# Attention: where the older unit's sums stand among the scores of a slot

## The chip, the core and the metric

One Trainium2 chip, one of its cores. The time is the device time in microseconds of one execution of the kernel; the median of three runs is compared.

## What is computed

Two macaron layers over a sequence of 2048 rows of 256 features, each a half-weighted feed-forward network, an attention with 16 heads of 16 features, and a second half-weighted feed-forward network. The change is in the attention, which both layers use. Cut to what matters (the first layer; the second has rotary positions and biases in place of the distance term):

```python
attn = jnp.einsum('bhqd,bhkd->bhqk', q, k) / math.sqrt(HEAD_DIM)
attn = attn + alibi_bias(seq_len, N_HEADS)[None] + causal_mask(seq_len)[None, None]
attn = jax.nn.softmax(attn, axis=-1)
y = jnp.einsum('bhqk,bhkd->bhqd', attn, v)
y = y.transpose(0, 2, 1, 3).reshape(bsz, seq_len, n_embd)
return jnp.einsum('bsd,de->bse', y, W_o)
```

## The kernel before

The sequence is cut into four chunks `c` of 512 queries, and the heads into four quartets `g`. A *group* `n = 4c + g` is one quartet's attention for one chunk of queries, so there are 16 groups in a layer. A *slot* is a group and a block `kb` of 128 keys. Group `n` has `4(c + 1)` slots, since later keys are masked: 4 slots for groups 0 to 3, 8 for 4 to 7, 12 for 8 to 11, 16 for 12 to 15, 160 in all. The last four slots of a group (`t` = 0 to 3) lie on the diagonal. There the first `128t` queries are left out and a mask is added by a further small matmul.

For a slot the kernel does this:

- `st_pair` (L725): scores with the keys on the partitions, two heads at a time, into a pair of PSUM banks (`pst`, L733). The matmuls are bf16 on the whole 128x128 array. There are two such pairs.
- `exp_pair` (L746): one exponential on ScalarE for two heads, into `pT` (L753). Five such tiles are held.
- `av_part` (L759): the sums. Each head's `pT` is multiplied with the values and a column of ones, in fp32, into a quarter of the partitions of one accumulator bank, `acc` (the tile `pav`, L768): a 128x32 piece of the array for each head. The 512 queries are cut at `mid` in two halves, `part` 0 and 1. A half is 8 instructions for the four heads. On the diagonal the halves are shorter, and for `t` = 2 and 3 all the queries are in `part` 0.
- After `part` 0 of a diagonal slot, `divide` (L779) transposes 128 finished columns of `acc` on VectorE (`yt`, L789), takes the reciprocals of the row sums (`rd`, L793) and multiplies on GpSimd (`zt`, L794).

The exponential needs the maximum of its row, which is worked out earlier, from scores with the queries on the partitions. That is done by `mx_unit` (L663): one matmul for each head (`pq`, L671, with a mask at L679 on the diagonal), into one of three PSUM buffers, and one VectorE reduction (`mx`, L682). A *maximum unit* is four heads of one block of 128 queries against 512 keys. The units belong to the next group, or to the one after it on the diagonal, and a hand-written plan (`put`, L837 to L859) spreads them over the slots. Nearly all slots have one, and some in the first chunk and at the start of a group have two; the last 19 slots of a layer have none. When a group's maxima are complete, `mx_end` (L684) and `mx_turn` (L699) bring them into rows of `q`, with three small DMAs.

The order on TensorE, ScalarE, VectorE and GpSimd is the order in which the program issues its instructions; each engine takes them one after the other and waits on semaphores. The loop at L939 writes this order. In a slot with a maximum unit it takes the head pairs in the order 1, 0 (`hp`). For each it issues two scores, two maximum scores with their reductions, the exponential, and then some sums:

```python
sums(i - 2 + (hp == 0), hp)
```

`sums(i, part)` (L929) issues every half that is waiting, up to this one. So behind heads 2,3 comes `part` 1 of the slot before the last, and behind heads 0,1 comes `part` 0 of the last slot. In a slot with no maximum unit both pairs' scores come first, then both exponentials, then `sums(i - 1, 1)`: both halves of the last slot. Further maximum units of the slot come after the sums (L966), then what is due (`run_due`: the turned maxima, the back-transpose `z`, the output matmuls `pwo`), and a step of the preparations (projections `pp`, `dn`, values `pv`) or of a layernorm of the neighbouring stage.

Of the kernel before, what the change touches and what calls it, by code (L numbers as in the profile page):

```python
# [46 lines left out]
def macaron_kernel(ctx: ExitStack, tc: tile.TileContext, a, out):  # L47
# [139 lines left out]
    def draw(work):  # L187
        while work and next(work[0], "end") == "end":
            work.popleft()

    def pull():

        for work in list(background)[:2]:
            if next(work, "end") == "end":
                background.remove(work)
# [294 lines left out]
    def attention(layer, following):  # L490
# [9 lines left out]
        with ExitStack() as st:  # L500
# [91 lines left out]
            def prep_v(c):  # L592
                ready(c)
                for t in range(0, T, 2):
                    pp = ps_one(f"pv{layer}_{c}_{t}").rearrange("p (t f) -> p t f", t=2)
                    for i in range(2):
                        for dc in range(DC):
                            nc.tensor.matmul(  # L598
                                pp[:, i, :],
                                lhsT=xns[c][:, dc, (t + i) * P : (t + i + 1) * P],  # L600
                                rhs=wqkv[:, dc, 2 * E : 3 * E],
                                start=dc == 0,
                                stop=dc == DC - 1,
                            )
                    for i in range(2):
                        vs = va[c][:, t + i, 0 : H * VW].rearrange("p (h d) -> p h d", d=VW)[:, :, 0:D]
                        pv = pp[:, i, :].rearrange("p (h d) -> p h d", d=D)
                        if layer == 0:
                            nc.scalar.copy(vs, pv)
                        else:  # L610
                            nc.vector.tensor_tensor(
                                vs, pv, b_v.rearrange("p (h d) -> p h d", d=D), ALU.add
                            )
                    if t + 2 == T:
                        done.add(("v", c))
                    yield
# [108 lines left out]
            def st_pair(n, kb, hp, apart=False):  # L725

                c, g = divmod(n, G)
                kc, t = divmod(kb, T)
                lo = t * P if kc == c else 0
                pair, ps = banks(f"pst{layer}_{n}_{kb}_{hp}", apart)  # L730
                for i in range(2):
                    hh = 2 * hp + i
                    nc.tensor.matmul(  # L733
                        ps[i][:, lo:CH],
                        lhsT=ks[n, kc][0:rows, hh, t * P : (t + 1) * P],
                        rhs=qs[n][0:rows, hh, lo:CH],
                        start=True,
                        stop=kc < c,
                    )
                    if kc == c:  # L740
                        nc.tensor.matmul(  # L741
                            ps[i][:, lo : lo + P], lhsT=ident_b, rhs=mask_kq, start=False, stop=True
                        )
                return pair, ps

            def exp_pair(n, kb, hp, scores):  # L746
                pair, ps = scores
                c, g = divmod(n, G)
                kc, t = divmod(kb, T)
                lo = t * P if kc == c else 0  # L750
                pT = ap.tile([P, 2, CH], F32, tag="pT", bufs=5, name=f"pT{layer}_{n}_{kb}_{hp}")
                if pair is not None:
                    nc.scalar.activation(pT[:, :, lo:CH], pair[:, :, lo:CH], AF.Exp, scale=0.25)  # L753
                else:
                    for i in range(2):
                        nc.scalar.activation(pT[:, i, lo:CH], ps[i][:, lo:CH], AF.Exp, scale=0.25)
                return pT

            def av_part(n, kb, pTs, part):  # L759
                c, g = divmod(n, G)  # L760
                kc, t = divmod(kb, T)
                lo = t * P if kc == c else 0
                mid = (lo + CH) // 2 if CH - lo > CH // 2 else CH
                a, b = ((lo, mid), (mid, CH))[part]
                if a < b:
                    for hh in range(4):
                        v0 = (4 * g + hh) * VW
                        nc.tensor.matmul(  # L768
                            acc[hh * SLOT : (hh + 1) * SLOT, a:b],
                            lhsT=va[kc][:, t, v0 : v0 + SLOT],  # L770
                            rhs=pTs[hh // 2][:, hh % 2, a:b],
                            start=kb == 0 and part == 0,
                            stop=kb == (c + 1) * T - 1,
                            skip_group_check=True,
                        )
                if part == 0 and kc == c:
                    divide(n, t)
# [89 lines left out]
            def run_due(all_of=False):  # L867
                while True:
                    due = [x for x in later if all_of or x[0] <= now[0]]
                    if not due:  # L870
                        return
                    later.remove(due[0])
                    due[0][1](*due[0][2])
# [3 lines left out]
            def step():  # L877
                draw(preps)

            def need(*what):  # L880
                while what not in done:
                    assert preps, what
                    step()
# [6 lines left out]
            def mx_next(unit, heads):  # L890
                n, t, kc = unit
                mx_unit(n, t, kc, heads)
                if 3 in heads:
                    left[n] -= 1
                    if not left[n]:
                        mx_end(n)
                        at(1, mx_turn, n)
# [8 lines left out]
            def load_to(slot):  # L906
                while uses and uses[0][1] <= slot:
                    load(*uses.popleft()[0])
# [12 lines left out]
            def turned(n):  # L921
                if n % 2 == 1:
                    c, q = divmod(n // 2, G // 2)
                    at(2, turn_back, c, q)
                    if q == G // 2 - 1:
                        for dc in range(DC):
                            at(3 + dc, output, c, dc)

            def sums(i, part):  # L929

                while unsummed and unsummed[0][::2] <= (i, part):
                    _, unit, p = unsummed.popleft()
                    n, kb, _ = unit
                    need("v", kb // T)
                    av_part(*unit, p)
                    if p == 1 and kb == (n // G + 1) * T - 1:
                        turned(n)

            for i, (n, kb) in enumerate(slots):  # L939
                c = n // G  # L940
                if kb == 0 and n % G == 0 and 0 < c < NCH - 1:

                    preps.extend((prep_qk(c + 1, "k"), prep_qk(c + 1, "q"), prep_v(c + 1)))
                if n not in turned_max:
                    run_due(all_of=True)
                load_to(i + 3)
                units = maxima.get(i, [])
                pTs = [None, None]
                if units:
                    for hp in (1, 0):  # L950
                        ps = st_pair(n, kb, hp)
                        mx_next(units[0], (2 - 2 * hp, 3 - 2 * hp))
                        pTs[hp] = exp_pair(n, kb, hp, ps)
                        sums(i - 2 + (hp == 0), hp)
                else:


                    both = []
                    for hp in (1, 0):
                        both.append(st_pair(n, kb, hp, pairs[0] % 3 == 2))  # L960
                        pairs[0] += 1
                    for hp, ps in zip((1, 0), both):
                        pTs[hp] = exp_pair(n, kb, hp, ps)
                    sums(i - 1, 1)
                unsummed.extend((i, (n, kb, pTs), part) for part in range(2))
                for unit in units[1:]:  # L966
                    mx_next(unit, (0, 1, 2, 3))
                run_due()
                if preps and (c <= 1 or i % 2):
                    step()  # L970
                    if c == 0 and i % 2:
                        draw(background)
                else:
                    pull()
                now[0] += 1
# [37 lines left out]
    def begin(layer, following):  # L1013
        att = attention(layer, following)
        begun[:] = att, next(att)
# [149 lines left out]
```

## Time and profile before

| what | value |
|---|---|
| three runs | 1952.93, 1954.04, 1957.03 us |
| their median | 1954.04 us |
| the profiled execution | 1957.69 us |
| its span, first to last instruction | 1955.7 us |
| granted TensorE clock, mean | 0.960 |
| attention of layer 0 and of layer 1, about | 266 to 789 us, 1203 to 1762 us |

The span is 2 us shorter than the execution's own time. PE is TensorE, DVE is VectorE, ACT is ScalarE, POOL is GpSimd. A row of the timeline has the start in us, the length in us, the engine, the line, the operation with output and inputs, how many instructions are merged in it, and in brackets the idle time before it with what ended it. Matmuls overlap, so that the distance from start to start counts for TensorE, and not the sum of lengths.

### The profile page before, as it was taken

Reading aid. Unit: us, or ns where it says so; the run is one execution under the profiler, and the core shown is the slowest. Engines: PE = TensorE matmul, PEld = TensorE weight load, DVE = VectorE, ACT = ScalarE, POOL = GpSimd, SP = SyncE. Lnnn points to the kernel's source line nnn. Section 1 sums busy time; section 2 is a strip of 40 time slices with the busy share of each in tenths; the row PEclk is TensorE's granted clock in tenths of the full one; section 3 lists DMA queues with packets and bytes.
Section 4 is the critical chain, followed back from the end, with each engine's and each line's share of the span. In section 5 each row is a group of like instructions: output and inputs, shape, how many; then the busy total and the mean of one; then the engine's idle time right before and its main releaser. Section 6 shows DMA issues by size and latency. Waiting matters only on the chain. (4 is left out here: it accounts for less than half of the span.)

```text
span 1955.7 us, 26994 instructions
## 1 busy us (share of the span) xinstructions
PE 1761.4 (90%) x10684; PEld 726.5 (37%) x10684; DVE 1361.6 (70%) x2384; ACT 894.2 (46%) x1112; POOL 458.4 (23%) x418
## 2 busy tenths in 40 slices
PE   5699789999999999789999876898999999998997
PEld 1233344433433333333444333433333333333443
DVE  7866377787788883666575655868877888825664
ACT  4343254555555668334422312445555656673220
POOL 3455321101000000455453432211111000003422
PEclk9799899999999999989999986999999999999999
DMA  4000252213211000200000115222122110000000
GB/s 129 1 1 33 82 148 83 73 54 102 62 45 46 28 28 2 73 1 0 1 11 0 54 61 158 82 73 92 52 69 86 43 43 26 18 1 0 11 11 22
DMA packets 50510, 93.10 MB, mean 48 GB/s; under 512 B 5424, under 2 KB 33072, under 8 KB 50128
## 3 DMA queue, kind: packets, MB, share of 16 engines
q1 hardware_dynamic: 49296, 89.28, 14.8%
q10 hardware_dynamic: 1088, 2.10, 0.3%
q8 instruction: 84, 1.38, 0.3%
q14 instruction: 42, 0.34, 0.1%
HBM read 59.51 MB, written 27.26 MB: 44 GB/s over the span
## 5 line engine op out<-in xcount | busy, mean ns | idle before, releaser
L682 DVE TENSOR_REDUCE mx<-pq 128x1 f32<-128x512 f32 (+3 forms) x1280 | 708.6, 603 | 158.5 <-PE pq L679 91.2
L753 ACT ACTIVATE pT<-pst 128x1024 f32<-128x1024 f32 (+3 forms) x614 | 542.6, 896 | 334.9 <-PE pst L733 196.8
L671 PE MATMUL pq<-k,q 105*128 105x512 bf16 (+7 forms) x1280 | 378.8, 353 | 74.7 <-DVE mx L682 52.3
L733 PE MATMUL pst<-q,k 99*128 99x512 bf16 (+7 forms) x1280 | 357.7, 354 | 5.1 <-ACT pT L753 4.2
L768 PE MATMUL pav<-pT,va 128*32 128x256 f32 (+1 forms) x4608 | 352.4, 382 | 5.2 <-DVE yt L789 5.0
L281 PE MATMUL pg_f<-xn,wgu 128*128 128x512 f32 x512 | 229.8, 602 | 11.5 <-DVE hr_f L318 11.5
L794 POOL TENSOR_TENSOR zt<-yt,rd 128x64 f32<-128x64 f32 x128 | 38.4, 300 | 795.2 <-DVE rd L793 795.1
L733 PEld LDWEIGHTS <-k 105*128 105x128 bf16 (+1 forms) x1280 | 101.5, 98 | 254.1 <-issue 218.4
L317 ACT ACTIVATE sl_f<-pg_f 128x512 f32<-128x512 f32 x128 | 76.0, 594 | 251.8 <-PE pg_f L281 175.0
L671 PEld LDWEIGHTS <-q 105*128 105x128 bf16 (+1 forms) x1280 | 124.5, 100 | 148.0 <-issue 44.3
L306 PE MATMUL pg_f<-xn,wgu 128*128 128x512 bf16 x512 | 156.2, 413 | 19.5 <-DVE wgu L170 6.8
L768 PEld LDWEIGHTS pav<-pT,va 128*32 128x32 f32 x4608 | 93.8, 108 | 208.7 <-issue 174.8
L281 PEld LDWEIGHTS pg_f<-xn,wgu 128*128 128x128 f32 x512 | 98.6, 193 | 136.9 <-issue 121.0
L306 PEld LDWEIGHTS <-wgu 128*128 128x128 bf16 x768 | 77.7, 101 | 166.9 <-issue 74.7
L292 PE MATMUL po_f<-h_f,wd 128*128 128x512 f32 x256 | 116.3, 608 | 17.3 <-DVE h_f L418 17.3
L340 POOL TENSOR_TENSOR ss_f<-ss_f,sq_f 128x512 f32<-128x512 f32 x56 | 91.1, 1628 | 111.5 <-ACT sq_f L339 111.3
L679 PE MATMUL pq<-mask_qk,ident_b 128*128 128x128 bf16 x512 | 107.3, 227 | 0.0
L741 PE MATMUL pst<-mask_kq,ident_b 128*128 128x128 bf16 x512 | 103.1, 222 | 0.0
L306 PE MATMUL pg_f<-xm_f,wgu 128*128 128x512 bf16 x256 | 85.3, 416 | 14.0 <-DVE xm_f L238 14.0
L318 DVE TENSOR_TENSOR h_f<-sl_f,pg_f 128x512 f32<-128x512 f32 x64 | 43.6, 682 | 76.4 <-ACT sl_f L317 76.3
L789 DVE STREAM_TRANSPOSE yt<-pav 128x128 f32<-128x128 f32 x128 | 39.8, 311 | 76.7 <-PE pav L768 76.7
L394 DVE TENSOR_TENSOR ge_f<-h_f 128x1536 bf16<-128x1536 f32 (+2 forms) x48 | 67.6, 1437 | 28.0 <-ACT h_f L387 28.0
(132 smaller groups left out, 1802.5 us busy)
## 6 DMA issues: line engine op xcount, KB each, us to landing
k<-dk SPq DMA_DIRECT2D x80, 384.0 KB
dk<-p_k SPq DMA_DIRECT2D x48, 256.0 KB
dq<-p_q SPq DMA_DIRECT2D x48, 256.0 KB
q<-dq SPq DMA_DIRECT2D x32, 384.0 KB
x<-in_xT ACTq DMA_DIRECT2D x4, 512.0 KB
raw<-in_w_gu SPq DMA_DIRECT2D x8, 256.0 KB
wgu<-in_w_gu SPq DMA_DIRECT2D x1, 2048.0 KB
cs_k<-in_cos_sin SPq DMA_DIRECT2D x4, 512.0 KB
```

The source lines that it names most:

```text
L281: nc.tensor.matmul(pg[:, half, :], lhsT=wgu[:, dc, half * F + f * P : half * F + (f + 1) * P], rhs=xn[:, dc, :], start=dc == 0, stop=dc == ...
L292: nc.tensor.matmul(po, lhsT=w[:, f, dc * P : (dc + 1) * P], rhs=h[:, f, :], start=f == 0, stop=f == FC - 1,)
L306: nc.tensor.matmul(pg[:, half, :], lhsT=wgu0[:, dc, half * F + f * P : half * F + (f + 1) * P], rhs=xp[part][:, dc, :], start=part == 0 an ...
L317: nc.scalar.activation(sl, pg[:, 0, :], AF.Silu)
L340: nc.gpsimd.tensor_tensor(ss, ss, sq, ALU.add)
L671: nc.tensor.matmul(pq, lhsT=qs[n][0:rows, hh, t * P : (t + 1) * P], rhs=ks[n, kc][0:rows, hh, 0:w], start=True, stop=kc < c,)
L679: nc.tensor.matmul(pq[:, w - P : w], lhsT=ident_b, rhs=mask_qk, start=False, stop=True)
L682: nc.vector.tensor_reduce(mxs[n][:, t, hh, kc : kc + 1], pq, AX.X, ALU.max)
L733: nc.tensor.matmul(ps[i][:, lo:CH], lhsT=ks[n, kc][0:rows, hh, t * P : (t + 1) * P], rhs=qs[n][0:rows, hh, lo:CH], start=True, stop=kc < c,)
L741: nc.tensor.matmul(ps[i][:, lo : lo + P], lhsT=ident_b, rhs=mask_kq, start=False, stop=True)
L753: nc.scalar.activation(pT[:, :, lo:CH], pair[:, :, lo:CH], AF.Exp, scale=0.25)
L768: nc.tensor.matmul(acc[hh * SLOT : (hh + 1) * SLOT, a:b], lhsT=va[kc][:, t, v0 : v0 + SLOT], rhs=pTs[hh // 2][:, hh % 2, a:b], start=kb == ...
```

## The change

In a slot with a maximum unit, no sums are issued between the two head pairs. After both pairs, their maxima and their exponentials, `sums(i - 1, 1)` issues both halves of the last slot's sums together, as in the slots with no maximum unit, which are left as they were. No instruction is added or taken away.

```diff
                         ps = st_pair(n, kb, hp)
                         mx_next(units[0], (2 - 2 * hp, 3 - 2 * hp))
                         pTs[hp] = exp_pair(n, kb, hp, ps)
-                        sums(i - 2 + (hp == 0), hp)
                 else:
-
 
                     both = []
                     for hp in (1, 0):
...
                     for hp, ps in zip((1, 0), both):
                         pTs[hp] = exp_pair(n, kb, hp, ps)
-                    sums(i - 1, 1)
+
+                sums(i - 1, 1)
                 unsummed.extend((i, (n, kb, pTs), part) for part in range(2))
```

## The prediction

> **What bounds the kernel now.** I read the page first, then the two attention stretches in the table by windows, then the timeline of single slots, and last the table of waits.
>
> ```profile
> PE 1761.4 (90%) x10684; PEld 726.5 (37%) x10684; DVE 1361.6 (70%) x2384; ACT 894.2 (46%) x1112; POOL 458.4 (23%) x418
> ```
>
> TensorE is busy for 90% of the span. In the windows of the two attention stretches (266 to 789 us, 1203 to 1762 us) it is fuller still; the last quarter of layer 0 reads:
>
> ```profile
> 611.00:789.00 178.00, 173.69 (x1520) 62.97 (x1516) 120.03 (x227) 119.85 (x144) 4.70 (x16) 1.00 0.08 23
> ```
>
> The columns after the length are PE, PEld, DVE, ACT and POOL busy, then the granted clock (1.00). PE has 173.7 of 178 us; VectorE 120. So what changes PE's own sequence changes the time. Here is one half of an undisturbed slot, on the timeline:
>
> ```profile
> 728.21 0.59 PE L671 MATMUL pq<-k,q 105*128 105x512 bf16 x2
> 728.41 1.02 ACT L753 ACTIVATE pT<-pst 128x1024 f32<-128x1024 f32 x1 [0.46 <-PE pst L733]
> 728.62 1.29 DVE L682 TENSOR_REDUCE mx<-pq 128x1 f32<-128x512 f32 x2 [0.25 <-PE pq L671]
> 728.73 0.64 PE L768 MATMUL pav<-pT,va 128*32 128x256 f32 x8
> 729.30 0.61 PE L733 MATMUL pst<-q,k 105*128 105x512 bf16 x2
> ```
>
> Two maximum scores (pq), eight pav instructions (one half of a unit's sums), two scores (pst). PE never waits: a half takes 1.54 us, a slot 3.08. VectorE has 0.25 us to spare in each half. From starts: pq to pav 0.52, pav to the next pst 0.57.
>
> **The change part by part.** No instruction is added or removed; no DMA, and no position in SP's queue, is touched. In a slot with a maximum unit, the half behind heads 2,3 goes, and behind heads 0,1 both halves of the unit one slot older stand together. Three things follow on PE and one on VectorE.
>
> *1. Fewer changes between score and sum matmuls: a gain.* The last group's slots (no maxima) already have both halves together:
>
> ```profile
> 759.31 1.07 PE L768 MATMUL pav<-pT,va 128*32 128x256 f32 x16
> ...
> 760.32 1.04 PE L733 MATMUL pst<-q,k 105*128 105x512 bf16 x4
> ```
>
> Sixteen pav instructions take 1.01 us to the next pst, two times eight take 2 x 0.57 = 1.14: 0.13 saved. The first slot of each group has no sums behind its first pair today, so it shows pq followed by pst:
>
> ```profile
> 662.86 0.59 PE L671 MATMUL pq<-k,q 105*128 105x512 bf16 x2
> ...
> 663.28 2.48 DVE L682 TENSOR_REDUCE mx<-pq 128x1 f32<-128x512 f32 x4 [0.19 <-PE pq L671]
> 663.29 0.59 PE L733 MATMUL pst<-q,k 105*128 105x512 bf16 x2
> 663.73 0.67 PE L671 MATMUL pq<-k,q 105*128 105x512 bf16 x2
> ```
>
> pq to pst is 0.43 in place of 0.52: 0.09 more. Together 0.22 a unit. Units off the diagonal with two halves, summed in slots with maxima: groups 4-7 have 4 each, 8-11 have 8, 12-14 have 12, so 84 a layer, 168 in all: **-37.0 us**. The Trainium skill, "TensorEngine Tiling (Array Packing)", section Key Properties, gives the reason: a change of tiling mode drains TensorE, and pav is 128x32 where the scores are 128x128. By that rule alone, the 56 diagonal units with two halves would gain 0.22 too, and the kernel about 49 us.
>
> *2. The fourth maximum score waits for its PSUM buffer: a loss.* pq has three buffers, so the fourth pq of a slot needs the slot's first reduction to be over. With sums in between it comes 2.2 us after the slot's start. In the burst it comes at 1.52, and the first reduction (start 0.85, 0.69 long) ends at 1.54. The row at 663.73 shows it: 0.67 for the two, not 0.59. 0.08 in each full-width slot; groups 4-14 have 62 of them a layer (kb 2 to the last before the diagonal; the masks of diagonal slots give the reduction time): 124 x 0.08 = **+9.9 us**.
>
> *3. On the diagonal the second half waits for VectorE: a loss.* After the first half of a diagonal unit `divide` puts a transpose of the accumulator on VectorE, and the second half is made to wait for it, though its columns are others. The last group shows it:
>
> ```profile
> 783.22 0.64 PE L768 MATMUL pav<-pT,va 128*32 128x256 f32 x8
> ...
> 784.00 0.32 DVE L789 STREAM_TRANSPOSE yt<-pav 128x128 f32<-128x128 f32 x1 [25.11 <-PE pav L768]
> ...
> 784.37 0.64 PE L768 MATMUL pav<-pT,va 128*32 128x256 f32 x8 [0.51 <-DVE yt L789]
> ...
> 785.72 0.53 PE L768 MATMUL pav<-pT,va 128*32 128x192 f32 x8
> ...
> 786.76 0.53 PE L768 MATMUL pav<-pT,va 128*32 128x192 f32 x8 [0.51 <-DVE yt L789]
> ```
>
> From one half to the next 1.15 us at t=0 and 1.04 at t=1, with VectorE idle. In the slots with maxima the transpose is queued behind the slot's four reductions. How long that is can be read where four reductions already run in a burst before it:
>
> ```profile
> 317.60 0.64 PE L768 MATMUL pav<-pT,va 128*32 128x256 f32 x8
> ...
> 318.46 0.31 DVE L789 STREAM_TRANSPOSE yt<-pav 128x128 f32<-128x128 f32 x1
> ```
>
> 318.46 plus the 0.37 between 784.00 and 784.37 is 318.83: 1.23 us after the half's start. Today the second half comes half a slot later, when the transpose is nearly or quite done, so this wait is almost unseen (DVE yt holds PE for 5.0 us in the whole run). At t=0 a unit costs today 2 x (0.57 + 0.09) = 1.32, then 0.09 + 1.23 + 0.57 = 1.89: +0.57. At t=1 the halves are 192 wide (0.47) and the reductions short, so the 1.04 stands: from 1.12 to 1.60, +0.48. 1.05 for a group; groups 4-13 have it, in two layers: 20 x 1.05 = **+21.0 us**. (Group 14's diagonal has no maxima and is together already.)
>
> Here a rule speaks against the change: the skill's "PSUM — Partial Sum Buffer", section Terms, lets no two engines be at one bank and quadrant at once. By it alone every second half has to come after the transpose; the rows agree, and they say what it costs.
>
> Groups 0-3 (all diagonal, in part with eight pq a slot) are worked out apart. Where VectorE sets the pace, PE's wait still starves it: in the slot at 301.96 the extra four pq would start at 305.93 and not at 304.60, and the reductions 0.92 later. For group 2 I get +0.9, group 3 +1.1, group 0 between 0.9 and 2.0 (I take 1.5), group 1 about 0 (the exponentials are late there anyway). The sum is 3.5 a layer; layer 1 was not worked out apart and is taken to be like it. With 0 and 8 as the ends for each layer: **+7.0 us**.
>
> *4. VectorE's other work loses its cover: a loss.* Subtractions of the projections (`dn`), layernorm pieces and the back-transpose `z` stand between a slot's reductions and the next one's. In the slot at 453.48 a 0.69 us subtraction puts the first reduction 1.43 us after the start, not 0.85. Today nothing is lost (3.07 us), as the pq that needs the buffer comes at 2.2. In the burst it waits until 1.43 + 0.69 + 0.05 = 2.17, where 1.60 was counted: +0.57. Some 14 slots off the diagonal are like that (5 with `dn` and 1 with a layernorm piece in layer 0, about 6 in layer 1, 2 with `z` and no output matmuls near), at about 0.5: **+7 us**. Ends: 0, if VectorE's idle 0.5 us a slot takes them; 20, a third of the 60 us of such work in groups 4-14.
>
> ScalarE loses nothing: a score buffer is needed again 1.2 us after its exponential ends. The sums' operands come free earlier, and one 0.42 us wait for them in group 14 goes (-0.8 for both layers). POOL's `zt` follows the transposes and holds up nobody.
>
> Sum: -37.0 + 9.9 + 21.0 + 7.0 + 7 - 0.8 = +7.1, call it **+7 us**.
>
> **Against which time.** The profiled execution took 1957.69 us (span 1955.7), 3.65 above the median of 1954.04 and 0.66 above the slowest of the three runs (1952.93 to 1957.03). The sum is a difference within it, 1957.69 to about 1965; carried to the median it gives 1961.0. About 0.2%, 3.9 us, is what a measurement of this kernel can tell from no change.
>
> **The rivals.**
> - *The drain wins.* Losses 2 and 4 vanish (VectorE catches up in the 0.5 us it has), and in groups 0-3 VectorE hides the waits. Then -37 + 21 - 0.8 = -17, or with loss 2 kept -7: 1937 to 1947. For it: VectorE is busy 120 of 178 us. Against: the 0.67 row, and that the 1.04 to 1.15 us of the diagonal are seen with VectorE idle, so no spare time there can help. Chance 0.15.
> - *It cancels.* Part 4 near 0 and groups 0-3 near 2 us a layer: within 4 us of 1954. Chance 0.20.
> - *VectorE becomes the bound in the middle groups.* Place: groups 4-11, where projections, layernorms and values run beside. A slot there offers 2.4 us of reductions to a period of 2.9. It decides once the other work in a slot is over 0.5 us; in some 30 slots a layer it is. At 0.5 each that is +30, in place of +7: about 1980. Against: half of these slots have 1.8 us of projection matmuls beside. Chance 0.10.
> - *The forecast*, +4 to +20: chance 0.55.
>
> **How the numbers follow.** Slower by over 0.2%: 0.55 + 0.10 = 0.65; within: 0.20; faster: 0.15. The likeliest case's own range is 1958 to 1974. For 8 in 10 I take 1947 to 1974: it holds the forecast, the cancelling case and the near edge of the drain's.
>
> **What would show it.** After: pav groups of 16 in the full slots, slots of 2.91 us in place of 3.08, and L768 waits for DVE yt of 0.5 to 0.9 us, some 56 more times (5.0 to some 30 us in the waits). "PE pq <- DVE mx" (52.3 us, 90 times today) goes up by 10 to 30 us. If the diagonal slots t=1 and t=2 (3.1 to 3.3 and 2.60 us today) do not grow to about 3.7 to 3.9 and 3.0, part 3 is wrong; if the full slots stay at 3.08, part 1 is; if slots with `dn` or `z` shorten like the others, part 4 is.

## The result and the profile after

| | before | changed |
|---|---|---|
| median of 20 runs each, side by side | 1956.14 us | 1961.51 us |
| profiled execution (span) | 1957.69 us (1955.7) | 1962.96 us (1961.0) |

The ratio is 1.0028, with a 95% interval of 1.0018 to 1.0037: slower by 5.4 us, between 3.5 and 7.2. In the two profiles the attentions, from a layer's first score matmul to its last, grew by 0.4 us in layer 0 and 2.2 in layer 1; the other 2.6 us of the 5.2 between the spans lie outside them, where the edit changes nothing. In the page of the changed kernel TensorE's busy time is lower, and the span is longer:

```profile
PE 1733.7 (88%) x10684; PEld 758.2 (39%) x10684; DVE 1350.2 (69%) x2384; ACT 882.7 (45%) x1112; POOL 456.2 (23%) x418
```

The window from 611 to 789 us of the changed kernel, columns as before, says the same: PE has work for 171.05 of 178 us, where it had 173.69, and VectorE has no more work than before.

```profile
611.00:789.00 178.00, 171.05 (x1570) 71.45 (x1570) 119.79 (x237) 118.53 (x148) 4.99 (x17) 1.00 0.08 23
```

A full slot off the diagonal, on the timeline of the changed kernel:

```profile
697.06 0.60 PE L733 MATMUL pst<-q,k 105*128 105x512 bf16 x2
697.50 0.59 PE L671 MATMUL pq<-k,q 105*128 105x512 bf16 x2
697.70 1.95 ACT L753 ACTIVATE pT<-pst 128x1024 f32<-128x1024 f32 x2 [0.96 <-PE pst L733]
697.92 2.48 DVE L682 TENSOR_REDUCE mx<-pq 128x1 f32<-128x512 f32 x4 [0.43 <-PE pq L671]
697.94 0.59 PE L733 MATMUL pst<-q,k 105*128 105x512 bf16 x2
698.37 0.67 PE L671 MATMUL pq<-k,q 105*128 105x512 bf16 x2
...
698.97 1.07 PE L768 MATMUL pav<-pT,va 128*32 128x256 f32 x16
699.98 0.39 PE L733 MATMUL pst<-q,k 105*128 105x512 bf16 x1
```

From 697.06 to the next slot at 699.98 it takes 2.92 us, where it took 3.08. Sixteen pav instructions take the 1.01 us that the last group showed, and the second pair of maximum scores is 0.67 long and not 0.59: the second score of this pair waits for its buffer. VectorE's idle time before a slot's reductions is 0.43 in one piece, where it was 0.25 twice.

On the diagonal it is given back. In the kernel before, the second half of a unit came 1.35 us after the first, with two scores and two maximum scores between, and the transpose was over by then (group 10 of layer 0, the unit of t = 0):

```profile
567.90 0.64 PE L768 MATMUL pav<-pT,va 128*32 128x256 f32 x8
568.47 0.28 PE L733 MATMUL pst<-q,k 105*128 105x256 bf16 x1
...
568.72 0.31 DVE L789 STREAM_TRANSPOSE yt<-pav 128x128 f32<-128x128 f32 x1
...
569.25 0.64 PE L768 MATMUL pav<-pT,va 128*32 128x256 f32 x8
```

In the changed kernel the slots t = 1 and t = 2 of group 13, in which the units of t = 0 and t = 1 are summed, read:

```profile
703.29 0.34 PE L733 MATMUL pst<-q,k 105*128 105x384 bf16 x1
...
704.17 1.95 DVE L682 TENSOR_REDUCE mx<-pq 128x1 f32<-128x384 f32 x4
...
705.18 0.64 PE L768 MATMUL pav<-pT,va 128*32 128x256 f32 x8
706.04 0.30 DVE L789 STREAM_TRANSPOSE yt<-pav 128x128 f32<-128x128 f32 x1
...
706.40 0.64 PE L768 MATMUL pav<-pT,va 128*32 128x256 f32 x8 [0.58 <-DVE yt L789]
...
707.17 0.28 PE L733 MATMUL pst<-q,k 105*128 105x256 bf16 x1
...
708.64 0.53 PE L768 MATMUL pav<-pT,va 128*32 128x192 f32 x8
709.31 0.32 DVE L789 STREAM_TRANSPOSE yt<-pav 128x128 f32<-128x128 f32 x1
...
709.68 0.53 PE L768 MATMUL pav<-pT,va 128*32 128x192 f32 x8 [0.51 <-DVE yt L789]
...
710.14 0.23 PE L733 MATMUL pst<-q,k 105*128 105x128 bf16 x1
```

The first half starts at 705.18, the transpose stands behind the four reductions at 706.04, and the second half is released only at 706.40. These two slots take 3.88 and 2.97 us, where they took 3.34 and 2.60. The table of waits of the changed kernel (total us, times, longest) counts 66 such waits of PE, where before there were 10 with 5.0 us:

```profile
PEld pav L768 <- DVE yt L789: 61.7, 64, 1.3
...
PE pq L671 <- DVE mx L682: 55.8, 100, 8.1
...
PE pav L768 <- DVE yt L789: 34.4, 66, 0.7
```

The waits of 0.58 and 0.51 us in these rows are a little less than the starts give. From half to half it is 1.22 us in place of the 0.57 that a half takes, 0.65 more, and 1.04 in place of 0.47, 0.57 more. A matmul row runs on to its modelled end, so the starts are the safer reading.

Slot by slot the two profiles differ by -1.1 us in group 13 of layer 0 (twelve units off the diagonal), -0.4 in group 11 (eight), +0.3 in group 7 (four) and +1.1 in group 3 (none).

### The profile page after: what moved, and what is told of

Read it like the earlier page. It is cut to its first block, busy times and chain, and to the rows that moved or that the text cites. A ratio compares the mean times of both kernels' runs of the same rounds, so it can differ in the third digit from the quotient of the medians.

```text
span 1961.0 us, 26992 instructions
## 1 busy us (share of the span) xinstructions
PE 1733.7 (88%) x10684; PEld 758.2 (39%) x10684; DVE 1350.2 (69%) x2384; ACT 882.7 (45%) x1112; POOL 456.2 (23%) x418
## 5 line engine op out<-in xcount | busy, mean ns | idle before, releaser
L682 DVE TENSOR_REDUCE mx<-pq 128x1 f32<-128x512 f32 (+3 forms) x1280 | 692.7, 602 | 165.2 <-PE pq L679 104.9
L753 ACT ACTIVATE pT<-pst 128x1024 f32<-128x1024 f32 (+3 forms) x614 | 531.2, 896 | 320.6 <-PE pst L733 184.6
L671 PE MATMUL pq<-k,q 105*128 105x512 bf16 (+7 forms) x1280 | 391.5, 353 | 78.5 <-DVE mx L682 55.8
L768 PE MATMUL pav<-pT,va 128*32 128x256 f32 (+1 forms) x4608 | 320.3, 381 | 34.6 <-DVE yt L789 34.4
L768 PEld LDWEIGHTS pav<-pT,va 128*32 128x32 f32 x4608 | 111.4, 109 | 233.4 <-issue 123.0
L733 PEld LDWEIGHTS <-k 105*128 105x128 bf16 (+1 forms) x1280 | 112.0, 98 | 195.8 <-issue 127.6
```

The lines of the kernel that those rows point to most:

```text
L671: nc.tensor.matmul(pq, lhsT=qs[n][0:rows, hh, t * P : (t + 1) * P], rhs=ks[n, kc][0:rows, hh, 0:w], start=True, stop=kc < c,)
L682: nc.vector.tensor_reduce(mxs[n][:, t, hh, kc : kc + 1], pq, AX.X, ALU.max)
L733: nc.tensor.matmul(ps[i][:, lo:CH], lhsT=ks[n, kc][0:rows, hh, t * P : (t + 1) * P], rhs=qs[n][0:rows, hh, lo:CH], start=True, stop=kc < c,)
L768: nc.tensor.matmul(acc[hh * SLOT : (hh + 1) * SLOT, a:b], lhsT=va[kc][:, t, v0 : v0 + SLOT], rhs=pTs[hh // 2][:, hh % 2, a:b], start=kb == ...
```

## The experiments

Theory A is the sum of the prediction: putting halves together gains on every unit, and a diagonal unit loses more than that, because its second half waits for the transpose. Rivals B, C and D stand with the runs that tell them apart. All six kernels were timed in five rounds against the kernel before, with 4 to 6 executions each and 14 of the fifth. The ratio is taken over all executions, and "faster" or "slower" in us is worked out from it; the difference of the two medians can be up to some 3 us away from that.

**Only the units off the diagonal together**

```diff
 (kernel before)
-                        sums(i - 2 + (hp == 0), hp)
+                        whole_unit = i > 0 and slots[i - 1][1] // T < slots[i - 1][0] // G
+                        sums(i - 2 + (hp == 0), 1 if whole_unit else hp)
```

> Only the units off the diagonal have both halves together (behind the second head pair); the diagonal units keep a half behind each pair, as in the kernel before. Theory A (the sum of the prediction: fewer changes between score and sum matmuls gain 37.0 us, the fourth maximum score loses 9.9, VectorE's other work 1 to 7, and the rest of the loss is the diagonal): 20 to 26 us faster than before, ratio 0.987 to 0.990. Rival B (the diagonal has little to do with it; the gain is eaten in all slots by VectorE's backlog and the three buffers): within 5 us of the kernel before, ratio 0.997 to 1.004, and full slots at about 3.0 us in place of 2.91.

Measured: 1933.28 us against 1952.81, ratio 0.9884 (0.9863 to 0.9904), 22.7 us faster (18.7 to 26.8). Full slots are at 2.91 us. Theory A stands and rival B falls: the gain off the diagonal has the size that A gave it, and VectorE's backlog and the three buffers do not eat it.

**Only the diagonal units together**

```diff
 (kernel before)
-                        sums(i - 2 + (hp == 0), hp)
+                        whole_unit = i > 0 and slots[i - 1][1] // T == slots[i - 1][0] // G
+                        sums(i - 2 + (hp == 0), 1 if whole_unit else hp)
```

> Only the diagonal units have both halves together; all others keep a half behind each pair, as before. Theory A: the waits of the second half for the transpose alone, 20 x 1.05 us in groups 4 to 13 and about 7.8 us in groups 0 to 3: 25 to 30 us slower than before, ratio 1.013 to 1.016, with 'PEld pav <- DVE yt' at about 60 us as in the changed kernel. Rival B: the half that waits is made good by the shorter next slot: within 5 us of before.

Measured: 1986.5 us against 1952.81, ratio 1.0165 (1.0143 to 1.0187), 32 us slower (28 to 37). That is a little more than Theory A's 25 to 30, and its interval reaches that range; rival B falls. Its waits and the place of one on its timeline:

```profile
PEld pav L768 <- DVE yt L789: 61.1, 64, 1.3
...
PE pav L768 <- DVE yt L789: 33.8, 66, 0.7
```

```profile
715.61 0.64 PE L768 MATMUL pav<-pT,va 128*32 128x256 f32 x8
716.43 0.31 DVE L789 STREAM_TRANSPOSE yt<-pav 128x128 f32<-128x128 f32 x1
...
716.79 0.64 PE L768 MATMUL pav<-pT,va 128*32 128x256 f32 x8 [0.55 <-DVE yt L789]
```

Two edits, one of 22.7 us gain and one of 32 us loss, make the change: 9.5 us slower by their sum, 5.4 measured, each part with an interval of about 4 us to either side. So the small result is a large gain and a larger loss.

**The transpose after both halves**

```diff
 (changed kernel, av_part)
-                if part == 0 and kc == c:
+                if kc == c and part == (mid < CH):
                     divide(n, t)
```

> The changed kernel, but divide (transpose, reciprocal, multiplication) is issued after the second half of a diagonal unit and not between the two halves. Theory A: the 1.05 us of 20 groups, the 7.8 us of groups 0 to 3 and the 0.5 us waits of groups 14 and 15 go, and the 56 diagonal units gain 0.22 each: 32 to 42 us faster than before, ratio 0.979 to 0.984; L768 hardly waits for yt. Rival C (the wait only moves: the next unit's sums now wait for a later transpose, or VectorE's later transposes delay the reductions by as much): at most 10 us faster than before.

Measured: 1923.61 us, ratio 0.9839 (0.9821 to 0.9858), 31 us faster than before. The same slots of group 13 on its timeline:

```profile
690.46 1.07 PE L768 MATMUL pav<-pT,va 128*32 128x256 f32 x16
691.35 0.39 PE L704 MATMUL ptm<-ident_b,neg 128*12 128x128 bf16 x4
691.67 0.32 DVE L789 STREAM_TRANSPOSE yt<-pav 128x128 f32<-128x128 f32 x1 [0.27 <-PE pav L768]
...
693.13 0.86 PE L768 MATMUL pav<-pT,va 128*32 128x192 f32 x16
694.12 0.32 DVE L789 STREAM_TRANSPOSE yt<-pav 128x128 f32<-128x128 f32 x1 [0.30 <-PE pav L768]
```

The sixteen are in one piece, the transpose follows, and no later sums wait for it: PE's waits for yt fall from 34.4 to 1.2 us. Theory A's range was 32 to 42 us, so the size is at its low edge; rival C, a wait that only moves, falls. Here the cause of the loss is taken away by itself, with both halves still together. About 4 us of it come from groups 14 and 15, where both halves stood together before the change too and waited for the transpose.

**The maxima first, in all slots with a maximum unit**

```diff
 (changed kernel)
-                    for hp in (1, 0):
-                        ps = st_pair(n, kb, hp)
-                        mx_next(units[0], (2 - 2 * hp, 3 - 2 * hp))
-                        pTs[hp] = exp_pair(n, kb, hp, ps)
+                    mx_next(units[0], (0, 1))
+                    both = [st_pair(n, kb, hp) for hp in (1, 0)]
+                    mx_next(units[0], (2, 3))
+                    for hp, ps in zip((1, 0), both):
+                        pTs[hp] = exp_pair(n, kb, hp, ps)
```

> The changed kernel, with the order of a slot's matmuls turned so that the fourth maximum score comes later after the first reduction's start: two maximum scores, all four scores, two maximum scores, sums. Theory A: the 0.08 us wait for the PSUM buffer in 124 full slots goes, with about the same in slots with other VectorE work: 8 to 12 us faster than the changed kernel, so 3 to 7 us faster than before (ratio 0.996 to 0.999), full slots 2.83 us. Rival D (the slot's length is set by the four reductions and their start, not by the buffer): full slots stay at 2.91 and the time at 1.002 to 1.003 of before.

Measured: 1966.32 us against 1952.81, ratio 1.0069 (1.0048 to 1.0089): slower than the changed kernel, against both theories. The full slots do what A said, but the total does not. One full slot of it:

```profile
691.59 0.61 PE L671 MATMUL pq<-k,q 105*128 105x512 bf16 x2
692.01 2.58 DVE L682 TENSOR_REDUCE mx<-pq 128x1 f32<-128x512 f32 x4 [0.25 <-PE pq L671]
692.03 1.03 PE L733 MATMUL pst<-q,k 105*128 105x512 bf16 x4
...
692.89 0.59 PE L671 MATMUL pq<-k,q 105*128 105x512 bf16 x2
693.42 1.07 PE L768 MATMUL pav<-pT,va 128*32 128x256 f32 x16
694.42 0.39 PE L671 MATMUL pq<-k,q 105*128 105x512 bf16 x1
```

2.83 us, and the second pair of maxima is 0.59 again, not 0.67: the wait for the buffer is gone. But the first slot of a group, which has two maximum units and is paced by VectorE, grew by 0.4 to 1.0 us in groups 5 to 11, and the second slot of some took 1 to 3 us more than in the kernel before. For group 11 of layer 1 the windows of this kernel (first slot, second slot, those after; the clock is the number after POOL's, third from the end) read:

```profile
1556.80:1561.80 5.00, 3.70 (x20) 1.13 (x19) 4.96 (x10) 1.94 (x2) 0.58 (x2) 0.96 0.45 142
1561.80:1567.20 5.40, 5.40 (x25) 1.64 (x24) 2.84 (x6) 1.94 (x2) 0.00 (x0) 0.50 0.01 3
```

In the first slot VectorE is busy for 4.96 of 5.00 us and PE for 3.70; in the second the granted clock is 0.50, and the slot takes 5.39 us, where it took 3.05 before and 3.48 in the changed kernel. Over layer 1's attention the mean clock is 0.95, where it was 0.97 before.

The stretches at half clock account for the miss. By the granted clock in the traces, 75 us of the two attentions run at half speed here, and 41 us in the changed kernel, as in the kernel before. The slots that no such stretch touches, in this profile and in that of the changed kernel, are 13.3 us shorter here, a little more than A's 8 to 12; the 29 others are 14.4 us longer. At full clock even the first two slots of a group gain together: 7.90 us in groups 7 and 11 of layer 0, for 8.11. So the longer first slot is made good in the second, and what costs is the half clock that falls on these slots. This is no accident of one profile: the six executions of this kernel have mean clocks of 0.948 to 0.952, the twenty of the changed kernel 0.957 to 0.963. Why this order brings such stretches about no run shows.

**The maxima first, only off the diagonal from kb = 2 on, with one maximum unit**

```diff
 (changed kernel)
+                    if len(units) == 1 and 2 <= kb < c * T:
                         (the five lines of the run before)
+                    else:
                         (the loop over hp, as in the changed kernel)
```

> The changed kernel, with the order of the run before (two maximum scores, four scores, two maximum scores, sums) only in the slots off the diagonal from kb = 2 on that have one maximum unit; all other slots as in the changed kernel. Theory A (the fourth maximum score's wait for its buffer costs 0.08 us in each such slot; what the order cost in the run before came from the first two slots of a group and from those with two maximum units): about 120 slots at 2.83 us in place of 2.91, 8 to 10 us faster than the changed kernel, ratio to before 0.997 to 0.999. Rival D (the total does not follow the slots, since what is gained comes back outside them): ratio 1.002 to 1.007, as in the run before.

Measured: 1954.91 us against 1954.86, ratio 0.9997 (0.9987 to 1.0006). Against the changed kernel's 1.0028 that is 6 us faster, by two ratios that were not measured side by side. It is below A's 8 to 10, and its interval reaches A's range; rival D falls. In the profiles the slots that are at full clock in both are 9.8 us shorter than in the changed kernel, which is in A's range. Its slots are at 2.83 us, and the first slots of the groups are as in the changed kernel.

**Both: the transpose last, and the maxima first in those slots**

> Both: divide behind the second half of a diagonal unit, and the order with the maxima first in the same slots off the diagonal. Theory A: the two gains add, 0.984 and 8 to 10 us: 38 to 42 us faster than before, ratio 0.978 to 0.981. Rival D: no better than divide alone, 0.983 to 0.986.

Measured: 1914.42 us against 1954.86, ratio 0.9789 (0.9773 to 0.9805): 41 us faster than the kernel before, and the fastest of all. The edit is that of the third run with that of the fifth. The gains add, within the intervals, as A had it.

## Why the prediction was right

The forecast was 1961.0 us, 7 slower than the median of then; the measured difference is 5.4 (3.5 to 7.2). A gain off the diagonal and a larger loss on it and in groups 0 to 3 were forecast, and the first three runs show both. That the two numbers lie so close is in part luck, for two reasons. The sum gives a full slot 0.22 less 0.08, so 2.94 us; the 2.91 that the prediction names as its sign, and that was measured, is 0.03 better, for 124 slots. With it the sum is +3.4 us and not +7.1. And in the two profiles the attentions grew by only 2.6 us: groups 0 to 3 by 7.9 (7.0 in the sum), groups 4 to 11 by 2.6 (the terms give about 7), groups 12 to 15 by -7.8 (about -7). The other 2.6 us, outside the attentions, stand in no term, and whether they come with the change no run shows. The terms, one by one:

- *1, the gain of 37.0, less 2, the buffer wait of 9.9.* Right in kind, and 0.03 us a slot too small. Full slots went from 3.08 to 2.91. The first run has these two, the operands' 0.8 and part 4 alone: 22.7 us measured. With -37.0 + 9.9 - 0.8 = -27.9, some 5 us are left for part 4, 1 to 9 by the interval. The fourth and fifth run take the wait of part 2 away and show the 0.08 (2.91 to 2.83). That the gain comes from the change of tiling mode, the reason given, no run shows: the sums differ from the scores in type (fp32 and bf16) as well as in tile. Of the operands' 0.8 nothing is seen: ScalarE's wait of 0.42 us in group 14 is gone, but its slot went from 3.28 to 2.85, which is only what the half that left it took.
- *3, the diagonal, 21.0 and 7.0.* Right. From half to half 1.22 us at t=0 and 1.04 at t=1 (1.23 and 1.04 were predicted from rows of the profile before). Groups 0 to 3 lose 4.2 us in layer 0 and 3.6 in layer 1, for 3.5. By itself the part costs 32 us (28 to 37) for 28. Why the wait stands there, though the columns are others, no run shows; that it is ordered so, and goes when the transpose is issued later, the third run shows.
- *4, VectorE's other work, 7.* The size is covered but not settled: 5 us by the first run with the sum's own terms, 8 with full slots at 2.91, and about 4, an estimate, from the 2.6 us of groups 4 to 11 in the two profiles. Of its steps one was right and one not. The `dn` step was right. In the slot that answers to the one at 453.48:

```profile
459.47 0.69 DVE L545 TENSOR_TENSOR dn_k<-pp_k,p_k 128x512 f32<-128x512 f32 x1 [2.21 <-ACT p_k L544]
459.51 0.59 PE L733 MATMUL pst<-q,k 105*128 105x512 bf16 x2
460.07 2.47 DVE L682 TENSOR_REDUCE mx<-pq 128x1 f32<-128x512 f32 x4
460.21 0.38 PE L671 MATMUL pq<-k,q 105*128 105x512 bf16 x1
460.81 0.38 PE L671 MATMUL pq<-k,q 105*128 105x512 bf16 x1 [0.22 <-DVE mx L682]
```

The reductions wait for the subtraction, the last pq waits for the first reduction until 2.16 us after the slot's start at 458.65 (2.17 was predicted), and the slot takes 3.47 us, for 3.07. But the `z` slots were put at 0.5 and cost 0.08 (2.99 us, where a full slot takes 2.91).

One sign failed: the waits "PE pq <- DVE mx" were to go up by 10 to 30 us, and went from 52.3 to 55.8. The wait of part 2 lies inside the row of 0.67 us, where this table does not count it.

One step was missed. The list of the change said that sums move, and not that what hangs on them does: with the last unit's second half popped a slot earlier, the back-transpose and the output matmuls come one slot earlier (`z` of group 10 in slot kb=3, not kb=4; the output matmuls of group 12 lengthen slot 3 by 1.7 us and shorten slot 5 by 2.0). In groups 10 and 12 that cost under 0.1 us.

The rival in which the drain wins, 7 to 17 us faster, is out by the total, and by its terms: the buffer wait stands in the full slots (0.67), the `dn` slot lost 0.40, and groups 0 to 3 lost 7.9. The rival in which the middle groups become VectorE's is not there either: groups 4 to 11 of layer 0 changed by +0.1 us in sum, and those of layer 1 by +2.5, where it had some 30. The rival in which it cancels is nearer than its chance of 0.20 says: its edge was 4 us, the interval begins at 3.5, and of its terms only the 2 us a layer for groups 0 to 3 are plainly wrong.

## What to carry to other kernels

When a change moves the time little, do its halves alone: here a gain of 23 us and a loss of about 32 were one edit. Check a sum by the place of its terms too: the total came out, the middle groups did not. Before two pieces of work are put together, ask what the program issues between them: the transpose had been free because half a slot lay behind it, and moving that one call behind both pieces turned a loss of 5 us into a gain of 31. An order that gains where TensorE sets the pace can bring half-speed stretches in the slots where VectorE does, and it can be chosen slot by slot.

## What the runs showed of the hardware that was not expected

A slot in which VectorE paces the matmuls can be followed by matmuls at half speed, in the changed kernel too. In group 10 of layer 1 the rows go from 0.22 to 0.43 us from score to score, and the windows give the clock:

```profile
1515.50:1520.10 4.60, 3.60 (x21) 1.24 (x20) 4.35 (x10) 2.05 (x2) 0.29 (x1) 1.00 0.28 98
...
1521.20:1524.60 3.40, 3.40 (x21) 1.07 (x20) 2.95 (x5) 1.62 (x2) 0.00 (x0) 0.52 0.00 0
```

PE was busy for 3.60 of the 4.60 us before, with no gap of over 0.7 us, and then had 0.52 of the clock for 3.4 us; the slot took 4.73 us, where the same slot of group 11 took 3.48. In the 3.41 us just ahead of the stretch PE had work for 2.30. Such stretches fall in other places in other profiles, and last 3.4 us or a multiple of it in all eight (one at the very end of a trace apart), so that a single slot's time should be read beside its clock. The Trainium skill, "TensorE: Matmul & The Clock Gate", Part 1: The HAM clock gate, has a gate that goes to half rate after an idle window of about 3.4 us; the length of the stretch agrees with that window, but here PE was not idle for one.
